# New planner ranks, an earlier first input and an early Tanh table in a four-layer kernel on one Trainium2 core

## The chip, the core and the metric

The kernel runs on one core of one Trainium2 chip. The metric is the device time of one execution in microseconds (us); lower is better. The time of before is the median of three runs.

The core's engines have queues of their own and meet through semaphores: TensorE (PE, matmuls and transposes), VectorE (DVE), ScalarE (ACT), GpSimd (POOL) and SyncE (SP, which here issues nearly all transfers).[...]

## What is computed

32 batches of a 256 x 256 block x pass through four layers. All numbers are fp32.

```python
# layer 0: a block conditioned on a scalar t
h = silu(noise_encoding(t) @ W1 + b1) @ W2 + b2
scale, shift = h @ Wsc + bsc, h @ Wsh + bsh
o = silu(scale * layer_norm(x, gamma, beta) + shift) @ W_in + b_in      # norm over the whole block
x = silu(scale * layer_norm(o, gamma, beta) + shift) @ W_out + b_out + x
# layer 1: attention, 16 heads of 16, with a bias [32, 16, 256, 256] and a key mask
x = ln(x) * (1 + ada_scale) + ada_shift                # ada from an integer token per batch
p = softmax(q @ k.T / 4 + attention_bias, masked)
x = x + (p @ v) @ Wo + bo
x = x + gelu2((ln(x) * g2 + beta2) @ W1 + b1) @ W2 + b2  # 256 -> 1024 -> 256
# layer 2: one step of a stencil equation: first and second differences along both axes
f = relu(f + dt * df)
# layer 3: causal attention of 16 heads, then a feed-forward with exact gelu, gated
y = x + gate * (transformer_block(x) - x)
```

## The kernel before

All weights stay on the chip. Each batch is worked on as two halves of 128 rows. One batch is some 390 matmuls and transposes for TensorE. An attention layer has four units of four heads: `scores` multiplies q and k of four heads in four row strips of the array (32 rows each, tile names sc <- k_t, nq), VectorE adds the bias or the causal mask and takes the minimum (pr, mn), ScalarE takes the exponential and its sum. `turned` transposes the probabilities (tr <- ident, pr), VectorE and ScalarE copy them out (pt). `values` multiplies them with v in four column strips (mm <- pt, L1v or L3v). A matmul thus runs in one of three shapes: the full array, 32 rows, or 32 columns. In layer 1 the bias (nb) comes in by 16 transfers per batch, and GpSimd subtracts it from the mask.

The order of work is not written out. A class `Order` (lines 69 to 383) records every operation of every batch first, with a rank, `order.now`, and its tiles. `arrange` then plans all engines at once with a table of costs: when an engine falls free, the ready operation with the lowest rank is taken. `emit` writes all engines' operations in the planned order, so every instruction of the recorded part bears line 382. The chip keeps that order on each engine.

What sets the ranks: `trace` (line 1155) walks a batch's layer as a generator and advances `order.now` by the yielded steps times `PACE`, starting from `b * PERIOD + START[layer] + EDGE.get((b, layer))` (line 1169), and adds `SHIFT[layer][step]` for each step. What else sets the choice: `EARLIER` moves TensorE operations by the kind of their output tile (line 252); `STAY` (line 302) is added to an operation that would change the array's shape; `FRESH` (line 306) is added on top when that change leads to a two-pass matmul (any fp32 matmul that is not a transpose) on the full array; `CAPS` limits the PSUM tiles of each kind in flight; `SLACK` (line 375) is a time that the plan adds before TensorE may use another engine's result.

```python
                    if e == "pe" and units[u][2][0]["length"][1] != shape:
                        rank += self.STAY
                        if units[u][2][0]["length"][1] != (P, P):
                            rank -= self.PAIR if shape != (P, P) else 0.0
                        elif units[u][2][0]["length"][3] == 2:
                            rank += self.FRESH
```

The plan's `TABLES` tells which function table ScalarE needs: Sin; Tanh and Exp together; Gelu.

The prologue (lines 542 to 652) has rank -1000: it loads the constants through SyncE's queue in the order of the code, computes the sine and cosine encodings on VectorE and ScalarE, and from them the conditioning of all 32 batches in three chained products (`conditioning`, line 606: a matmul group, a copy, a transpose, an addition of the bias): W1 with a silu, W2, then scale and shift (wss). Bias vectors are loaded as rows (as_rows) and transposed. The first batch's x is loaded at line 559, behind W2 and wss. `layer_0` (line 990) takes the block's mean and variance with two one-column matmuls (`block_stats`, line 759), then the scaled silu and two products.

Of the kernel before, what the change touches and what calls it, by code (L numbers as in the profile page):

```python
# [16 lines left out]
AF = mybir.ActivationFunctionType  # L17
# [21 lines left out]

PERIOD = 86.0
START = (-61.8, 0.0, 116.9)
PACE = (1.55, 1.23, 1.08)
EDGE = {(0, 0): 14.4, (0, 1): -5.0, (0, 2): 5.8, (1, 0): -19.0, (1, 1): -3.8, (1, 2): -0.2, (2, 0): -27.1, (2, 1): -2.0, (2, 2): -1.1, (3, 0): 12.3, (3, 1): 0.4, (3, 2): 0.3, (4, 0): 5.2, (4, 1): 2.3, (4, 2): 0.6, (27, 0): -1.1, (27, 1): -1.0, (27, 2): 0.5, (28, 0): 1.7, (28, 1): -0.3, (28, 2): -2.0, (29, 0): 2.1, (29, 1): -0.1, (29, 2): -2.1, (30, 0): -11.1, (30, 1): 5.7, (30, 2): -4.5, (31, 0): -16.9, (31, 1): 1.9, (31, 2): 15.4}
SHIFT = (
    {0: -93.0, 1: -33.6, 2: -27.5, 3: -32.8, 4: -14.7, 5: -56.4, 6: -42.3, 7: -28.3, 8: 23.1},
    {0: -9.7, 1: -80.2, 2: -10.3, 3: -1.7, 4: 2.7, 5: 8.8, 7: -7.0, 8: 14.7, 9: -90.2, 11: 7.3,
     12: 21.2, 13: -0.4, 14: 4.0, 15: -1.3, 16: 11.4, 17: 5.1, 19: 4.8, 20: 10.4, 21: 46.1, 22: 16.4,
     23: -8.7, 24: -13.1, 25: -30.4, 26: -2.4, 27: -90.0, 28: 8.3, 29: -134.0, 30: -0.4, 31: -13.2,  # L50
     32: -34.6, 33: 0.8, 34: -0.3, 35: 7.7, 36: -2.9, 37: -8.0},
    {0: -1.1, 1: -32.9, 2: -9.3, 3: 27.2, 4: 23.9, 5: -25.6, 6: -48.6, 7: -36.4, 8: -12.9, 9: 6.6,
     11: 3.0, 12: 15.4, 13: -32.5, 15: -6.5, 16: 20.0, 17: -2.0, 18: 6.6, 19: -0.5, 20: 0.4, 21: -82.2,
     23: 9.0, 24: 7.5, 25: 0.1, 26: -11.0, 27: -38.3, 28: 12.2, 29: 7.0, 30: 30.4, 31: 3.6, 32: -8.7,
     33: -46.1, 34: 4.4, 35: 2.3, 36: -58.5, 37: -16.3, 38: -59.7, 39: 18.0, 40: -15.2, 41: 12.6},
    {0: -24.5, 1: -13.3, 2: 6.7, 3: -84.2, 4: 42.8},
)
NORM = 8.0
LAND = 3.0
# [5 lines left out]
class Order:  # L65
# [11 lines left out]
    TURN = 92.0  # L77
    FIRST = {(32, P): 107.0, (P, 32): 27.0, (P, P): 107.0}
    APART = 120.0
    SLACK = 50.0  # L80
    SEEN = {(32, P): 165.0, (P, 32): -16.0, (P, P): 165.0}
    CAPS = {"sc": 8, "tr": 7, "mm": 7}
    EARLIER = {"sc": 29.6, "mm": -2.0, "tr": 6.2}
    STAY = 5.0
    FRESH = 1.0
    PAIR = 0.0
    PORT = 0.05
    TABLES = {AF.Sin: 0, AF.Tanh: 1, AF.Exp: 1, AF.Gelu: 2}
# [128 lines left out]
    def arrange(self):  # L217
# [5 lines left out]
        turns = defaultdict(list)  # L223
        room = dict(self.CAPS)
        first = {}
        for u, (engine, rank, xs) in enumerate(units):
# [6 lines left out]
            for t in {t.name: t for x in xs for t in x["tiles"]}.values():  # L233
                f = first.setdefault(t.name, u)
                if f == u:
                    room[t.tag] = t.bufs or t.tag_meta.bufs
                    count[t.tag] += 1
                    if t.source_name in self.CAPS:
                        count[t.source_name] += 1
# [10 lines left out]
        for u, (engine, rank, xs) in enumerate(units):  # L250
            name = next((t.source_name for x in xs for t in x["tiles"] if t.source_name in self.CAPS), "")
            ranks.append((rank - (self.EARLIER.get(name, 0.0) if engine == "pe" else 0.0), u))
        for us in turns.values():
# [15 lines left out]
        def may(u, at):  # L269
            ready_at[u] = max(ready_at[u], at)  # L270
            wait[u] -= 1
            if not wait[u]:
                heapq.heappush(coming[units[u][0]], (ready_at[u], u))
                heapq.heappush(events, ready_at[u])
# [6 lines left out]
        while todo:  # L281
# [6 lines left out]
            for e in self.ENGINES:  # L288
# [6 lines left out]
                for k, heap in ready[e].items():  # L295
# [5 lines left out]
                    if e == "pe" and units[u][2][0]["length"][1] != shape:  # L301
# [3 lines left out]
                        elif units[u][2][0]["length"][3] == 2:  # L305
                            rank += self.FRESH
                    if k[1]:
# [66 lines left out]
                for v in after[u]:  # L374
                    may(v, own if units[v][0] == e and x["method"] != "dma_start" else end + self.HOPS[units[v][0]] + (self.SLACK if units[v][0] == "pe" else 0.0))

# [54 lines left out]
def kernel(ctx: ExitStack, tc: tile.TileContext, io, out, n_batch=B):  # L431
    nc = tc.nc
    order = Order()
    pe, dve, act, pool, sync = (
        order.engine(name, eng)
        for name, eng in (
            ("pe", nc.tensor), ("dve", nc.vector), ("act", nc.scalar), ("pool", nc.gpsimd), ("sync", nc.sync)
        )
    )
# [17 lines left out]
    def rows(ap):  # L457

        return ap.rearrange("(c p) n -> p c n", p=P)
# [37 lines left out]
    def mm_tile(shape):  # L497
        return psum_tile(shape, "mm")
# [22 lines left out]
    def turned_vectors(tag, names, eng):  # L521
        vectors, n_rows = {}, 0
        for name in names:
            n = io[name].shape[0] // P
            vectors[name] = slice(n_rows, n_rows + n)
            n_rows += n
        as_rows = sb.tile([n_rows, P], F32, tag="nq0", name="as_rows")
        for name, at in vectors.items():
            eng.dma_start(as_rows[at], io[name].rearrange("(c p) -> c p", p=P))
        pm = mm_tile([P, n_rows])  # L530
        pe.transpose(pm, as_rows, ident[0:n_rows, 0:n_rows])
        cols = ctile(tag, [P, n_rows])
        dve.tensor_copy(cols, pm)
        return cols, {name: cols[:, at] for name, at in vectors.items()}

    def load_x(b):
        x = sb.tile([P, C2, D], F32, tag="x", name="x")
        sync.dma_start(x, rows(io["x"][b]))
        return x
# [9 lines left out]
    )  # L549
    w1 = sb.tile([P, 4 * E], F32, tag="t2", name="l0w1", bufs=3)  # L550
    sync.dma_start(w1, io["L0_cond_W1"])
    i_b = sb.tile([P, B], I32, tag="nq1", name="i_b")
    sync.dma_start(i_b, io["itok_B_34_63"].partition_broadcast(P))
    w2 = sb.tile([P, 4, 4 * E], F32, tag="hid", name="l0w2", bufs=1)
# [1 line left out]
    wss = sb.tile([P, 2, 4, D], F32, tag="pt", name="l0wss", bufs=3)  # L556
    sync.dma_start(wss[:, 0], rows(io["L0_cond_Wsc"]))
    sync.dma_start(wss[:, 1], rows(io["L0_cond_Wsh"]))
    first_x = load_x(0)
    gb = []  # L560
    for n in ("gamma", "beta"):
        t = sb.tile([P, C2, D], F32, tag="l2", name="l0gb", bufs=4)
# [16 lines left out]
    def cosine(dst, a, r, parts=slice(0, P)):  # L579

        dve.tensor_scalar(a, r, -1.0, None, ALU.mult)
        dve.tensor_tensor(a, a, r, ALU.max)
        dve.tensor_scalar(a, a, -1.0, math.pi / 2, ALU.mult, ALU.add)
        act.activation(dst[parts], a[parts], AF.Sin)

    small = sb.tile([P, 16, B], F32, tag="pr", name="encodings", bufs=10)
    x0, r0, n0, a0, enc, x1f, r1, n1, a1, emb0, emb1 = (small[:, i] for i in range(11))
# [8 lines left out]
    reduced(r1, n1, x1f)  # L596
    act.activation(emb0, r1, AF.Sin)
    cosine(emb1, a1, r1)

    def silu(dst, zh, th, z):  # L600

        dve.tensor_scalar(zh, z, 0.5, None, ALU.mult)
        act.activation(th, zh, AF.Tanh)
        dve.scalar_tensor_tensor(dst, th, 1.0, zh, ALU.add, ALU.mult)

    def conditioning(dst, weights, src, bias):


        pm = mm_tile([P, P])
        with order.together():  # L610
            for k in range(len(weights(0))):
                for j in range(4):
                    pe.matmul(
                        pm[j * B : (j + 1) * B, :], lhsT=src[:, k, :], rhs=weights(j)[k],
                        start=k == 0, stop=k == len(weights(0)) - 1,
                    )
        by_batch = sb.tile([P, P], F32, tag="h_t", name="by_batch")
        dve.tensor_copy(by_batch, pm)
        pm = mm_tile([P, 4, B])
        pe.transpose(pm.rearrange("p j b -> p (j b)"), by_batch, ident)  # L620
        dve.tensor_tensor(dst, pm, bias.unsqueeze(2).broadcast_to([P, 4, B]), ALU.add)
# [6 lines left out]
    part = lambda j: slice(j * P, (j + 1) * P)  # L628
    conditioning(h1, lambda j: [w1[:, part(j)]], enc.unsqueeze(1), vector["L0_cond_b1"])
    silu(h1s, zh, th, h1)  # L630
    conditioning(h2, lambda j: [w2[:, k, part(j)] for k in range(4)], h1s, vector["L0_cond_b2"])
    both = cols0[:, 8:12]
    conditioning(mod0, lambda j: [wss[:, j // 2, k, part(j % 2)] for k in range(4)], h2, both)
# [17 lines left out]
    sync.dma_start(parity, io["c_parity"])  # L651
    order.now = START[0] + 5.0
    _, more = turned_vectors(
# [501 lines left out]
    def trace(n, gen, layer, start, pace):  # L1155
        i = 0
        while True:
            order.now = start + SHIFT[layer].get(i, 0.0)
            step = next(gen, None)
            if step is None:  # L1160
                break
            start += step * pace
            i += 1

    trace(3 * n_batch, loads(), 3, START[1] + 25.0, 1.0)
    res = {}
    for b in range(n_batch):
        for i, layer in enumerate((layer_0, layer_1, layers_23)):
            trace(3 * b + i, layer(b, res), i, b * PERIOD + START[i] + EDGE.get((b, i), 0.0), PACE[i])
    with tc.manual_schedule():  # L1170
# [34 lines left out]
```

## Time and profile before

| | |
|---|---|
| median of three runs | 2665.15 us (2664.05 to 2667.85) |
| the profiled execution | 2665.54 us |
| its span, first to last instruction | 2663.7 us |
| mean granted TensorE clock | 0.989 of full speed |
| TensorE idle from 0 to 95 us | 34.2 us |
| TensorE idle from 300 to 2450 us | 2.4 us |
| TensorE idle in the last 64 us | 17.0 us |
| bytes moved | 169.69 MB, 64 GB/s in the mean, 207 GB/s over the first 95 us |

The profile comes from one execution. Times in its rows are in us. A row of the timeline gives the start from the beginning of the span, the length, the engine, the code line, the operation, the tiles written and read, the size and how many like it follow each other; a bracket tells idle time before it and what ended it. TensorE's rows overlap, because matmuls are pipelined: the distance from start to start is what one costs. A fp32 matmul that is not a transpose leaves two records. A row of the stretches gives the stretch, its length, then the busy time of PE, PE's weight loads, DVE, ACT and POOL with their counts, then the granted clock of TensorE, the busy share of the 16 DMA engines and GB/s.

### The profile page before, as it was taken

To read this page: it belongs to the slowest core of one execution; us is meant where nothing else is said; L and a number is where in the kernel's file an instruction comes from. 1 tells how busy PE (TensorE), PEld (TensorE's weight loads), DVE (VectorE), ACT (ScalarE), POOL (GpSimd) and SP (SyncE) were. 2 spreads that over 40 slices of the span, in tenths; PEclk is the share of its full clock that TensorE was granted. 3 is DMA by queue.
4 is the path that set the end of the run, shared out by engine and by line. 5 is a ranking of instruction groups with operands and counts; after the bars stand their busy time and mean duration, and the time that the engine had idled before them with its cause. 6 is when DMAs were issued, how large, how long until landed. Compare 5 with 4: busy or idle time off the path is not lost.

```text
span 2663.7 us, 60400 instructions
## 1 busy us (share of the span) xinstructions
PE 2600.2 (98%) x20462; PEld 2118.4 (80%) x20462; DVE 2122.1 (80%) x7627; ACT 1920.1 (72%) x6120; POOL 1565.0 (59%) x1960
## 2 busy tenths in 40 slices
PE   5999999999999999999999999999999999999997
PEld 4777888888888888888888888888888888888775
DVE  5887888878878877878878878877878887887853
ACT  2677777877777877777777777877777877777854
POOL 3865676555676555576555677555576555676420
PEclk7999999999999999999999999999999999999998
DMA  7321122212122212122212122212122211122100
GB/s 243 110 60 59 42 73 69 70 49 66 45 70 70 70 49 66 46 70 69 70 49 65 43 73 70 69 49 66 46 69 69 70 57 57 42 69 64 45 5 9
DMA packets 177064, 169.69 MB, mean 64 GB/s; under 512 B 19514, under 2 KB 175220, under 8 KB 176756
## 3 DMA queue, kind: packets, MB, share of 16 engines
q1 hardware_dynamic: 176720, 165.82, 20.2%
q8 instruction: 163, 2.67, 0.4%
q14 instruction: 145, 1.19, 0.1%
q10 hardware_dynamic: 36, 0.01, 0.0%
HBM read 157.40 MB, written 8.39 MB: 62 GB/s over the span
## 4 chain that ended last, share of the span: by engine, by line
PE 91%; DVE 3%; ACT 2%; DMA 1%; POOL 1%; issue 1%; SPq 0%; ACTq 0%; POOLq 0%; DVEq 0%
PE mm L382 68%; PE tr L382 14%; PE sc L382 9%; DVE pr L382 1%; ACT hid L382 1%; ACT pr L382 1%; DMA x<-in_x_dram 1%; POOL nb L382 0%; DMA nb<-in_fside_Bx16xSxS_dram 0%; DVE pt L382 0%; ACT L382 0%; POOL rstd L382 0%; DVE gd L382 0%; DMA L1wo<-in_L_cond_Wo_dram 0%; DVE st L382 0%
## 5 line engine op out<-in xcount | busy, mean ns | idle before, releaser
L382 ACT ACTIVATE pr<-pr,mn 128x256 f32<-128x256 f32 (+1 forms) x2048 | 966.9, 478 | 93.0 <-DVE mn L382 91.8
L382 POOL TENSOR_TENSOR nb<-mask_f,nb 128x512 f32<-128x512 f32 x512 | 693.3, 1378 | 114.7 <-DMA nb<-in_fside_Bx16xSxS_dram 101.9
L382 PE MATMUL tr<-ident,pr 128*128 128x128 f32 x3584 | 508.5, 276 | 5.4 <-ACT pr L382 1.8
L382 PEld LDWEIGHTS tr<-ident,pr 128*128 128x128 f32 x3584 | 419.5, 143 | 85.8 <-ACT pr L382 29.1
L382 DVE CUSTOM_DVE_ANT_0 pr<-sc,nb 128x256 f32<-128x256 f32 x1024 | 388.0, 414 | 25.3 <-POOL nb L382 14.0
L382 ACT ACTIVATION_READ_ACCUMULATOR pr<-pr,mn 128x1 f32 x2048 | 398.0, 194 | 0.0
L382 DVE COPY pt<-tr 128x512 f32<-128x512 f32 (+1 forms) x512 | 311.3, 615 | 72.9 <-PE tr L382 72.3
L382 POOL TENSOR_SCALAR hid<-hid 128x256 f32<-128x256 f32 x256 | 100.0, 405 | 433.4 <-ACT hid L382 433.1
L382 DVE CUSTOM_DVE_ANT_0 pr<-sc,causal 128x128 f32<-128x128 f32 (+1 forms) x1024 | 299.3, 352 | 38.5 <-PE sc L382 37.2
L382 PE MATMUL sc<-k_t,nq 32*128 32x256 f32 (+1 forms) x4096 | 269.5, 375 | 0.1
L382 ACT COPY pt<-tr 128x512 f32<-128x512 f32 (+1 forms) x512 | 261.4, 526 | 10.9 <-PE tr L382 6.0
L382 PE MATMUL mm<-L3w,hid 128*128 128x256 f32 x1024 | 241.5, 385 | 10.1 <-ACT hid L382 10.0
L382 PE MATMUL mm<-h_t,L3w 128*128 128x256 f32 x1024 | 247.6, 382 | 1.5 <-DVE h_t L382 1.4
L382 PE MATMUL mm<-h_t,L1w 128*128 128x256 f32 x1024 | 248.9, 381 | 0.0
L382 PE MATMUL mm<-L1w,hid 128*128 128x256 f32 x1024 | 239.0, 380 | 0.1
L382 PEld LDWEIGHTS sc<-k_t,nq 32*128 32x128 f32 x4096 | 163.3, 185 | 73.0 <-issue 25.7
L382 PEld LDWEIGHTS mm<-L3w,hid 128*128 128x128 f32 x1024 | 190.6, 193 | 35.1 <-ACT hid L382 11.9
L382 POOL COPY wide<-rs 128x256 f32<-128x256 f32 x128 | 53.3, 416 | 281.3 <-DVE rs L382 131.8
L382 PEld LDWEIGHTS mm<-L1w,hid 128*128 128x128 f32 x1024 | 186.6, 190 | 23.3 <-issue 1.2
L382 PEld LDWEIGHTS mm<-h_t,L3w 128*128 128x128 f32 x1024 | 184.2, 191 | 22.9 <-DVE h_t L382 2.5
L382 PEld LDWEIGHTS mm<-h_t,L1w 128*128 128x128 f32 x1024 | 183.7, 190 | 23.3 <-issue 1.8
L382 ACT ACTIVATE t<-x,shift,rstd 128x256 f32<-128x256 f32 x128 | 67.2, 590 | 148.8 <-DVE shift L382 148.8
(173 smaller groups left out, 4997.7 us busy)
## 6 DMA issues: line engine op xcount, KB each, us to landing
nb<-in_fside_Bx16xSxS_dram SPq DMA_DIRECT2D x512, 256.0 KB
x<-in_x_dram SPq DMA_DIRECT2D x32, 256.0 KB
out_dram<-d SPq DMA_DIRECT2D x32, 256.0 KB
mask<-in_mask_Bx1xSxS_bk_dram SPq DMA_DIRECT2D x32, 64.0 KB
L1w<-in_L_cond_W_dram SPq DMA_DIRECT2D x2, 1024.0 KB
L3w<-in_L_cond_W_dram SPq DMA_DIRECT2D x2, 1024.0 KB
l0w<-in_L_cond_W_dram SPq DMA_DIRECT2D x1, 1024.0 KB
g_b<-in_L_cond_B_grid_dram SPq DMA_DIRECT2D x3, 256.0 KB
```

Of the source, the lines that this page charges most:

```text
L382: call(*args, **kwargs)
```

## The change

Nothing in the computation changes. x of the first batch is loaded directly behind W1 instead of behind wss. One activation is added, a Tanh of one column behind the last cosine, whose output nobody uses. The second and third conditioning products, and what is recorded behind them in the prologue, get the rank -960 instead of -1000; layer 0 of the first batch gets about -1070 (its EDGE), so its statistics rank ahead of them. All other ranks are replaced, SLACK doubles, FRESH goes from 1 to 8, and the limits for score and other PSUM tiles fall by one. In the instruction orders that follow from it, every engine's queue is rearranged through all 32 batches; the number of instructions of each kind on each engine stays, but for that one activation, and the number of table loads on ScalarE is 65 in both.

```diff
-PERIOD = 86.0
-START = (-61.8, 0.0, 116.9)
-PACE = (1.55, 1.23, 1.08)
-EDGE = {(0, 0): 14.4, (0, 1): -5.0, (0, 2): 5.8, (1, 0): -19.0, (1, 1): -3.8, (1, 2): -0.2, (2, 0): -27.1, (2, 1): -2.0, (2, 2): -1.1, (3, 0): 12.3, (3, 1): 0.4, (3, 2): 0.3, (4, 0): 5.2, (4, 1): 2.3, (4, 2): 0.6, (27, 0): -1.1, (27, 1): -1.0, (27, 2): 0.5, (28, 0): 1.7, (28, 1): -0.3, (28, 2): -2.0, (29, 0): 2.1, (29, 1): -0.1, (29, 2): -2.1, (30, 0): -11.1, (30, 1): 5.7, (30, 2): -4.5, (31, 0): -16.9, (31, 1): 1.9, (31, 2): 15.4}
+PERIOD = 85.9
+START = (-60.6, 0.0, 116.2)
+PACE = (1.29, 1.23, 1.08)
+EDGE = {(0, 0): -1009.2, (0, 1): -5.2, (0, 2): 1.9, (1, 0): -49.5, (1, 1): -2.6, (2, 0): -9.3, (2, 1): -5.2, (2, 2): -0.7, (3, 0): 0.6, (3, 1): 0.5, (3, 2): -1.4, (4, 0): -18.2, (4, 1): 2.8, (4, 2): 0.6, (27, 0): -14.4, (27, 1): -6.5, (28, 0): -7.6, (28, 1): -3.2, (28, 2): -2.7, (29, 0): -18.9, (29, 1): 3.1, (29, 2): 30.9, (30, 0): 6.8, (30, 1): -0.5, (30, 2): 24.0, (31, 0): -17.2, (31, 1): 8.1, (31, 2): -22.4}
 SHIFT = (
...
 )
...
-    SLACK = 50.0
+    SLACK = 100.0
     SEEN = {(32, P): 165.0, (P, 32): -16.0, (P, P): 165.0}
-    CAPS = {"sc": 8, "tr": 7, "mm": 7}
-    EARLIER = {"sc": 29.6, "mm": -2.0, "tr": 6.2}
+    CAPS = {"sc": 7, "tr": 7, "mm": 6}
+    EARLIER = {"sc": 32.7, "mm": -1.2, "tr": 6.9}
     STAY = 5.0
-    FRESH = 1.0
+    FRESH = 8.0
...
     w1 = sb.tile([P, 4 * E], F32, tag="t2", name="l0w1", bufs=3)
     sync.dma_start(w1, io["L0_cond_W1"])
+    first_x = load_x(0)
     i_b = sb.tile([P, B], I32, tag="nq1", name="i_b")
...
     sync.dma_start(wss[:, 1], rows(io["L0_cond_Wsh"]))
-    first_x = load_x(0)
     gb = []
...
     cosine(emb1, a1, r1)
+    act.activation(a1[:, 0:1], emb1[:, 0:1], AF.Tanh)
...
     silu(h1s, zh, th, h1)
+    order.now = -960.0
     conditioning(h2, lambda j: [w2[:, k, part(j)] for k in range(4)], h1s, vector["L0_cond_b2"])
```

SHIFT is replaced in all its entries: four tables of 9, 35, 39 and 5 numbers that move a layer's steps by a few tens, for example step 21 of layer 1 from 46.1 to 142.1.

## The prediction

> **What bounds the kernel now.** I read the page's busy times first, then busy time by stretches of the span, then the timelines of TensorE and ScalarE in one steady batch, and last the timeline of TensorE at the end.
>
> The page, and the stretches (PE busy is the second number of a row):
>
> ```profile
> PE 2600.2 (98%) x20462; PEld 2118.4 (80%) x20462; DVE 2122.1 (80%) x7627; ACT 1920.1 (72%) x6120; POOL 1565.0 (59%) x1960
> ```
>
> ```profile
> 0.00:95.00 95.00, 60.78 (x415) 43.59 (x416) 58.26 (x219) 34.71 (x102) 47.00 (x64) 0.82 0.66 207
> ...
> 300.00:1200.00 900.00, 899.94 (x7156) 738.24 (x7155) 738.36 (x2666) 675.71 (x2155) 548.65 (x688) 1.00 0.20 61
> ...
> 2537.00:2664.00 127.00, 105.53 (x670) 81.84 (x668) 59.69 (x222) 62.30 (x196) 22.66 (x36) 0.90 0.02 7
> ```
>
> From 300 to 1200 us TensorE is idle for 0.06 us in 900. So two things can move the time: how long TensorE's own stream takes, and the gaps in it at both ends and wherever a new order opens one. No work is removed; the program has 12606 matmuls and transposes before and after.
>
> What one costs, I take from starts in the timeline of TensorE in a steady batch:
>
> ```profile
> 1187.63 1.03 PE L382 MATMUL mm<-L3wv,h_t 128*128 128x256 f32 x4
> 1188.59 0.94 PE L382 MATMUL sc<-k_t,nq 32*128 32x128 f32 x16
> 1189.45 1.13 PE L382 MATMUL mm<-L3wv,h_t 128*128 128x256 f32 x4
> 1190.52 0.94 PE L382 MATMUL sc<-k_t,nq 32*128 32x128 f32 x16
> 1191.38 0.66 PE L382 MATMUL mm<-ident,t 128*128 128x128 f32 x4
> 1191.88 0.49 PE L382 MATMUL tr<-ident,pr 128*128 128x128 f32 x3
> ...
> 1193.07 0.82 PE L382 MATMUL tr<-ident,pr 128*128 128x128 f32 x6
> ```
>
> A fp32 matmul of 256 columns shows as two records and follows the one before after 0.432 us when nothing changes. The two of the first row take 0.96, so going over from the full array (128*128) to a quarter of its rows (32*128) costs 0.093. The same two in the third row take 1.07: coming back costs another 0.104. A transpose takes 0.109 in a row of its kind and 0.165 as the first after a score or value group, so coming back to a transpose costs 0.056. These starts repeat within 2 ns over the run. With such spacings all 12606 instructions take 2558 us. I call the rest of the span, 105.4 us, lost; followed along the records, it is 53.6 at 95 us, 60.2 at 300, 64.6 at 2450, 67.2 at 2537 and 105.4 at the end.
>
> **The change, part by part. TensorE's order.** FRESH 1 to 8 makes the planner reluctant to come back from the small-tile shapes to a two-pass matmul; SLACK, CAPS, EARLIER and the new shifts rearrange the rest. I counted changes of shape in both instruction orders. Full array to score or value group: 327 before, 287 after, 40 x 0.093 = 3.7 us. Back to a two-pass matmul: 99 to 58, 41 x 0.104 = 4.3 us. Back to a transpose: 228 both times. Transpose to two-pass matmul, 0.0027 each: 727 to 619, 0.3 us. A one-column matmul (statistics) ahead of a transpose, 0.034: 57 to 36, 0.7 us; ahead of a two-pass matmul, 0.083: 65 to 64, 0.1. Together **-9.1 us**, all of it on the engine that is never idle.
>
> **One new wait per batch.** Now ScalarE in the same microsecond:
>
> ```profile
> 1185.01 1.07 ACT L382 ACTIVATE t<-xm,shift,rstd 128x256 f32<-128x256 f32 x2
> 1187.83 0.84 ACT L382 ACTIVATE k_t<-mm,cols 128x256 f32<-128x256 f32 x2 [1.75 <-PE mm L382]
> 1188.69 1.28 ACT L382 ACT_TABLE_LOAD   x1
> 1189.98 0.40 ACT L382 ACTIVATE pr<-pr,mn 128x128 f32<-128x128 f32 x1
> ...
> 1190.38 0.49 ACT L382 ACTIVATE pr<-pr,mn 128x256 f32<-128x256 f32 x1
> 1190.78 0.19 ACT L382 ACTIVATION_READ_ACCUMULATOR pr<-pr,mn 128x1 f32 x1
> ...
> 1191.77 0.51 ACT L382 ACTIVATE pr<-pr,mn 128x256 f32<-128x256 f32 x1
> ```
>
> Here the two t activations run before k_t, in an idle gap. In the changed order they stand between k_t and the table load in 21 batches, so every exponential behind them starts 1.07 us later. Behind them on ScalarE stand the load, four exponentials and two L3v copies; TensorE waits for the exponentials. The first transposes started at 1191.88, and the sum behind the second exponential had been read at 1190.78 + 0.19 = 1190.97: 0.91 to spare, so 0.16 short after. The transposes of the next tile (first at 1193.07) had their data at 1192.37 (exponential at 1191.77, its read 0.41 later, 0.19 long), 0.70 to spare; the changed order brings them 0.08 closer to the scores, so 0.70 - 0.08 - 1.07 = 0.45 short. A later wait in the same batch does not add, it is the same lateness. 21 x 0.45 = **+9.5 us**. Bounds: the lateness could vanish if the scores themselves come later (0), or grow by a second such place that I don't see (0.8 each): 0 to 17.
>
> This is where the Trainium skill speaks against the change. The row shows the load at 1.28 us and the exponential 0.01 later, with nothing after it. "ScalarE: Activation LUTs", section "What ACT_TABLE_LOAD costs", adds about 1.38 us of drain to every switch of the table. By the row the wait is 0.45 a batch; by the page it would be 0.45 + 1.38 = 1.83, since in the changed order an activation runs right up to the load (38 us in all). But k_t runs right up to it before as well, and no drain shows, so I take the row.
>
> **The prologue.** The added Tanh is one 128x1 activation, by the nearest row (64x32) 0.23 us. But it stands behind a Sin again: the changed order on ScalarE is Sin, Tanh (for the hidden layer), Sin, Tanh, four loads where two stood. The two added loads and the activation, 2 x 1.28 + 0.23 = 2.8 us, lie between the hidden layer's tanh (done at 11.6) and the next ScalarE work at 18.86, a gap of 7.2 us: nothing, and 2.8 at most if that gap were gone. (At the end two loads are saved, 65 in all both times.)
>
> x behind W1 costs no bytes; it moves SyncE's later issues by one, 0.43 us, and the 1 MB of W2 behind a wait for t_b's landing (4.18), 1.5 us later than now. x should land near 6 (W1 lands at 4.91, 256 KB more at 350 GB/s) instead of 12.90, so TensorE's wait of 2.47 us for it goes, and VectorE's statistics no longer hold back the hidden layer (11.05 to 12.90). What is late next: both gamma and beta now stand ahead of the W2 matmuls on TensorE, and beta lands around 14.4 (the second bias row's issue at 14.38 waits for it), so those matmuls start near 15.4 against 14.83. Then the bias rows (as_rows, 22.87 now, about 0.5 earlier since the second x was moved behind them) stand ahead of the transpose that gives the scale. The first input matmul (27.25) gains about 0.5 us. And after it the order is fixed: L1's Wo matmul, which waits for its transfer until 32.68, ahead of the means. The second x now travels ahead of Wo (0.7 us at the 360 GB/s of that stretch), so Wo lands no earlier. Hence the first stages keep their time; the gain is that 1.9 us more of TensorE's work (the second batch's input matmuls) stands ahead of the first L1 transposes at 50.17. **-2 us**; bounds -5 (the bias transfers of the first L1 attention, where 12 us are lost from 65 to 95, also fall better) and +4 (they fall worse; SyncE's queue there is reordered too). From 95 to 300 I take the 6.5 us lost as unchanged, +-4.
>
> **The end.** The last rows of TensorE before the change:
>
> ```profile
> 2599.81 1.89 PE L382 MATMUL mm<-h_t,L3wq 128*128 128x256 f32 x8
> ...
> 2628.59 2.56 PE L382 MATMUL mm<-L3wo,ctx_t 128*128 128x256 f32 x8
> 2634.88 0.93 PE L382 MATMUL mm<-ident,t 128*128 128x128 f32 x4 [3.73 <-ACT t L382]
> 2636.45 8.73 PE L382 MATMUL mm<-h_t,L3w 128*128 128x256 f32 x32 [0.64 <-DVE h_t L382]
> 2649.34 8.86 PE L382 MATMUL mm<-L3w,hid 128*128 128x256 f32 x32 [4.15 <-ACT hid L382]
> ```
>
> The last batch runs alone there: 24 us of the last 64 are lost. In the changed order, batch 30's last feed-forward (14.3 us of TensorE work) stands inside the last batch's attention. I take as milestone the end of the last batch's L1 Wo (2537.04), with 88.5 us of TensorE work left before and 96.0 after. The last batch's chain from there, in the changed order: two waits of 4.0 and 1.4 us to its feed-forward; 19.1 us of dense work and 1 us for the last gelu; 25.4 us to its L3 input transposes (22.6 now; VectorE's score work of batch 30 now stands in it); 2.2 to Q. That makes 53.1. Q to Wo takes 28.8 now, 30.5 with eight more ScalarE activations (0.42 each, half hidden). Wo to the first feed-forward matmul takes 7.9 now; batch 30's gelu with its table load (1.28 + 1.91) and 6.9 us of matmuls stand in it, 10.0. From there 27.2 now, 25.9 without a load of its own. Sum 119.5; with 1.5 for what I have overlooked, 121.0. That leaves 121.0 - 96.0 = 25.0 lost, against 126.7 - 88.5 = 38.2: **-13.2 us**. Bounds -19 and 0. On the way to the milestone the order is tighter than now (the first L1 feed-forward matmul stands right behind its input): +0.5, between 0 and 3.
>
> **Sum.** -9.1 + 9.5 - 2 + 0.5 - 13.2 = -14.3. The profiled execution took 2665.54 us (span 2663.7); the median of the runs shown is 2665.15, 0.4 below. 2665.15 - 14.3 = 2650.9, so 2651.
>
> **Rivals.** *The end gives nothing*: batch 30's ScalarE work (3.4 of bias activations, 3.2 of load and gelu) and VectorE work falls into the last batch's chain and costs the 13 us that TensorE gains. For it: both are serial there. Against it: ScalarE is busy 28 of the last 64 us. -1.1, 2664. *The ScalarE wait doesn't arise*, since small latenesses elsewhere already absorb it: -23.8, 2641. *The ScalarE wait is much longer*: one mechanism, the t activations and the load ahead of the first exponential in 21 batches. The other terms give -23.8, so it turns the result to slower by 0.2% from (23.8 + 5.3) / 21 = 1.39 us a batch; at the 1.83 of the drain it makes +14.6, 2680. For it: TensorE has no idle time that would take it up. Against it: the load row. *The change doesn't do what it says*: x early buys nothing, since Wo's landing decides; that is in my sum.
>
> **Numbers.** A measurement of this kernel can tell about 0.2%, 5.3 us, from no change. Forecast 0.58, end gives nothing 0.14, no wait 0.20, long wait 0.08. Faster by over 0.2% (below 2659.8): nearly all of the forecast, all of no wait and some of the first rival, 0.82; within: 0.12; slower: 0.06. The range runs from 2635 (no wait, and the end at its better bound) to 2664 (the end gives nothing).
>
> **What would show it.** TensorE's starts: 287 entries into small shapes at +0.093; if they cost differently, the first step is wrong. Around each third-layer attention, t between k_t and the table load, and transposes waiting about 0.45 for ACT pr; the row 300:1200 would then show some 5 us idle. Wo landing near 32.5 and the first L1 transposes near 50. 96 us of TensorE work in the last 121. The prediction is wrong if TensorE waits over 1 us per batch, or if the last batch's Q starts more than 72 us before the end.

## The result and the profile after

The median of 20 runs is 2671.64 us (2668.5 to 2676.18) against 2665.37 us for the kernel before in the same comparison: a ratio of 1.0024, 95% interval 1.0018 to 1.0030. The change makes the kernel slower by 0.24%, where the forecast was 0.5% faster. The profiled execution has a span of 2670.6 us (before 2663.7), a difference of 6.9 (7.0 in the table below, whose rows are rounded).

First the page's busy times, then the stretches of the span, in the columns of the rows of before:

```profile
PE 2612.4 (98%) x20462; PEld 2120.9 (79%) x20462; DVE 2130.2 (80%) x7627; ACT 1921.1 (72%) x6121; POOL 1553.7 (58%) x1960
```

```profile
0.00:95.00 95.00, 65.73 (x424) 44.87 (x425) 58.24 (x220) 37.39 (x106) 48.63 (x66) 0.82 0.65 208
...
300.00:1200.00 900.00, 896.22 (x7071) 732.65 (x7071) 737.74 (x2617) 661.77 (x2110) 540.69 (x681) 1.00 0.20 61
```

TensorE is idle for 3.8 us in the 900, against 0.06 before. That looks small. But look at the counts: 7071 records instead of 7156 in the same 900 us, although the new order's spacings are shorter. The busy column doesn't show where the time goes, because the drawn ends of matmuls are modelled and a drawn row covers most of a short pause.

The starts do show it. Take the spacings that the prediction read from the kernel before, lay them along each kernel's own order on TensorE, and call lost what is left over between one start and the next. Summed over the whole trace, this is the ledger:

| us | before | after | difference | predicted |
|---|---|---|---|---|
| TensorE's own stream (12606 instructions at their spacings) | 2558.3 | 2548.9 | -9.3 | -9.1 |
| lost from 0 to 300 | 60.2 | 61.1 | +0.9 | -2 |
| lost from 300 to 2450 | 4.4 | 35.5 | +31.1 | +9.5 |
| lost from 2450 to the end | 40.8 | 25.1 | -15.7 | -12.7 (the end -13.2, the way there +0.5) |
| sum | 2663.7 | 2670.6 | +7.0 | -14.3 |

One row is far off, and it is large enough to turn the sign. Of the 35.5 us in it, 24.3 are at one place, where the kernel before loses less than 0.1: the first three tiles of probability transposes (three transposes each) of the third-layer attention, nearly all of it in 19 batches. This is TensorE there, in the batch that stands for the one shown of before:

```profile
1198.49 1.03 PE L382 MATMUL mm<-L3wv,h_t 128*128 128x256 f32 x4
1199.45 0.94 PE L382 MATMUL sc<-k_t,nq 32*128 32x128 f32 x16
...
1202.86 0.33 PE L382 MATMUL tr<-ident,pr 128*128 128x128 f32 x1
1203.36 0.44 PE L382 MATMUL tr<-ident,pr 128*128 128x128 f32 x2 [0.16 <-ACT pr L382]
1203.63 1.03 PE L382 MATMUL mm<-h_t,L1wq 128*128 128x256 f32 x4
1204.50 0.98 PE L382 MATMUL tr<-ident,pr 128*128 128x128 f32 x4
1205.64 0.44 PE L382 MATMUL tr<-ident,pr 128*128 128x128 f32 x2 [0.16 <-ACT pr L382]
```

From 1202.86 to 1203.36 one transpose takes 0.50 where 0.11 is its spacing: 0.39 lost, of which the bracket calls 0.16 idle. It had itself started 0.12 late (4.37 behind the first row, 4.25 before). The six transposes that followed each other before now break after the fourth. From the first row to the fifth of them, at 1205.64, it takes 7.15; the kernel before did the same in 5.88 (1187.63 to 1193.51, which is the row at 1193.07 and four spacings of 0.109). So 1.27 us were lost on this way, and 0.06 behind it, since the transpose that follows a pause starts 0.06 late. The page's table of waits, restricted to 300 to 2450, has 5.0 us in 29 waits for these exponentials, and the ledger 24.3. The Trainium skill, "Perfetto Trace Analysis", section "Tensor Engine Instruction (MATMUL, LD_WEIGHTS)", says that TensorE's end in a trace is estimated. That fits what the rows show: a single transpose is drawn with 0.33 us where its spacing is 0.11, and four fifths of the waits show no idle time.

ScalarE and VectorE in the same microseconds:

```profile
1198.69 0.84 ACT L382 ACTIVATE k_t<-mm,cols 128x256 f32<-128x256 f32 x2 [1.97 <-PE mm L382]
1199.91 1.09 ACT L382 ACTIVATE t<-xm,shift,rstd 128x256 f32<-128x256 f32 x2 [0.38 <-DVE shift L382]
1201.02 1.28 ACT L382 ACT_TABLE_LOAD   x1
1202.32 0.40 ACT L382 ACTIVATE pr<-pr,mn 128x128 f32<-128x128 f32 x1
```

```profile
1199.01 0.68 DVE L382 SCALAR_TENSOR_TENSOR th<-th,y 128x512 f32<-128x512 f32 x1
1199.61 0.33 DVE L382 TENSOR_SCALAR shift<-mv,rstd 128x1 f32<-128x1 f32 x2
```

The order is the predicted one: k_t, t, load, exponentials. But t doesn't follow k_t directly. It waits 0.38 us for shift, which stands behind th on VectorE in the new order. The first exponential starts 3.83 us behind the first row of the TensorE block (1198.49), against 2.35 before (1189.98 less 1187.63): 1.48 us late, not 1.07.

Seven of the 19 batches are like this one. In eleven others shift comes earlier, t waits 0.15 us for it, and the first exponential is 1.25 us late (1282.67, with the TensorE block from 1279.07); one batch lies between.

```profile
1280.26 1.09 ACT L382 ACTIVATE t<-xm,shift,rstd 128x256 f32<-128x256 f32 x2 [0.15 <-DVE shift L382]
```

The last exponential that the six transposes need is the second of the third tile. Its sum is read here, in the kernel before and in the changed one (the batch shown first):

```profile
1193.06 0.19 ACT L382 ACTIVATION_READ_ACCUMULATOR pr<-pr,mn 128x1 f32 x1
```

```profile
1205.40 0.19 ACT L382 ACTIVATION_READ_ACCUMULATOR pr<-pr,mn 128x1 f32 x1
```

At the end the profile shows what was predicted, batch 30's feed-forward inside the last batch's attention:

```profile
2607.98 1.89 PE L382 MATMUL mm<-h_t,L3wq 128*128 128x256 f32 x8
...
2636.72 1.56 PE L382 MATMUL mm<-L3wo,ctx_t 128*128 128x256 f32 x6 [0.37 <-DVE ctx_t L382]
2639.49 5.45 PE L382 MATMUL mm<-L3w,hid 128*128 128x256 f32 x24 [1.20 <-ACT hid L382]
...
2656.88 8.79 PE L382 MATMUL mm<-L3w,hid 128*128 128x256 f32 x32 [2.87 <-ACT hid L382]
```

Where TensorE stood idle before between Wo and the last feed-forward (3.73 for t), it now does w2 of batch 30. From the end of the last batch's layer-1 Wo matmul (2552.25) the rest takes 118.4 us with 96.0 us of TensorE work in it.

### The profile page after: what moved, and what is told of

It reads as the page before. It is cut to its first block, busy times and chain, and to the rows that moved or that the text cites. A ratio compares the mean times of both kernels' runs of the same rounds, so it can differ in the third digit from the quotient of the medians.

```text
span 2670.6 us, 60377 instructions
## 1 busy us (share of the span) xinstructions
PE 2612.4 (98%) x20462; PEld 2120.9 (79%) x20462; DVE 2130.2 (80%) x7627; ACT 1921.1 (72%) x6121; POOL 1553.7 (58%) x1960
## 4 chain that ended last, share of the span: by engine, by line
PE 53%; POOL 17%; DVE 14%; ACT 8%; DMA 4%; issue 3%; SPq 1%; POOLq 0%; ACTq 0%; DVEq 0%
PE mm L382 38%; PE tr L382 9%; PE sc L382 6%; POOL nb L382 5%; ACT pr L382 4%; DMA nb<-in_fside_Bx16xSxS_dram 3%; POOL d L382 2%; POOL rstd L382 2%; DVE dd L382 2%; DVE pr L382 2%; DVE nq L382 1%; DVE x L382 1%; POOL offset L382 1%; ACT L382 1%; POOL cmf L382 1%
## 5 line engine op out<-in xcount | busy, mean ns | idle before, releaser
L382 PEld LDWEIGHTS tr<-ident,pr 128*128 128x128 f32 x3584 | 412.9, 142 | 103.1 <-ACT pr L382 46.1
L382 ACT ACTIVATION_READ_ACCUMULATOR pr<-pr,mn 128x1 f32 x2048 | 412.6, 201 | 0.0
L382 DVE DVE_READ_ACCUMULATOR2_ANT mn<- 128x1 f32 x2048 | 168.9, 82 | 0.0
```

Source lines behind the costliest of these rows:

```text
L382: call(*args, **kwargs)
```

## The experiments

Theory A: all of the surplus at the transposes is lateness of ScalarE's exponentials, made of t's length and t's wait for shift; what exceeds the spare of the tightest tile (the time by which its data are early) goes one to one into TensorE's wait. Rivals: something else in the new order, such as VectorE's minima or fewer matmuls between the transposes, sets the waits (theory B); or the prediction's own 0.45 us a batch holds and the rest comes from elsewhere.

Some edits are made behind the plan: `emit` sorts by the planned start, so changing the start of single operations moves these alone. Each experiment but the sixth and the tenth leaves TensorE's order through the steady part as it was. Ratios are to the kernel before, run in the same comparison.

**1. The table load taken out of the way.** A tiny exponential ahead of k_t makes ScalarE load the table in its idle gap.

```diff
+            elif func(x) == AF.Exp and table == AF.Gelu:
+                table, j = AF.Exp, i
+                while is_t(acts[j - 1]) or is_k(acts[j - 1]):
+                    j -= 1
...
+                    more.append({"call": (call, (self.tick[0], self.tick[1], AF.Exp), {}), "start": acts[j]["start"] - 0.01})
```

> The changed kernel with one 128x1 exponential added in 22 batches, ahead of k_t on ScalarE, where that engine waits 1.97 us for TensorE; its output is used by nobody. The table load then happens there and not behind t; all other instructions keep their order. Theory A (the waits of 1.24 us a batch at the first three groups of probability transposes come from ScalarE being late by t, its wait for shift, and the load): 1.28 of the 1.47 us of lateness go, the transposes wait for less than 0.1 us a batch, 2671.6 - 23 = 2648. Theory B (the waits are set by something else in the new order, VectorE's minima or the thinner cover of matmuls between the transposes): 2671, within 2 us. If the added load does not fit into the gap and delays k_t, some 0.3 us a batch come back: 2655.

Measured: 2646.65 us, ratio 0.9931 (0.9919 to 0.9944). Theory A holds, theory B falls, and 25 us less than the changed kernel is more than 0.45 us a batch could give back. ScalarE, then TensorE:

```profile
1182.77 1.28 ACT L400 ACT_TABLE_LOAD   x1
1184.06 0.20 ACT L400 ACTIVATE tick<-mhalf 128x1 f32<-128x1 f32 x1
1184.67 0.84 ACT L400 ACTIVATE k_t<-mm,cols 128x256 f32<-128x256 f32 x2 [0.40 <-PE mm L400]
1185.75 1.09 ACT L400 ACTIVATE t<-xm,shift,rstd 128x256 f32<-128x256 f32 x2 [0.24 <-DVE shift L400]
1186.74 0.39 ACT L400 ACTIVATE pr<-pr,mn 128x128 f32<-128x128 f32 x1
```

```profile
1184.47 1.03 PE L400 MATMUL mm<-L3wv,h_t 128*128 128x256 f32 x4
...
1188.71 0.49 PE L400 MATMUL tr<-ident,pr 128*128 128x128 f32 x3
...
1189.91 0.82 PE L400 MATMUL tr<-ident,pr 128*128 128x128 f32 x6
```

The load and the tick fill 1.5 us in which ScalarE was waiting for TensorE anyway. k_t still starts when TensorE has it. The six transposes follow without a pause. From 300 to 2450, 11.4 us are lost instead of 35.5. This kernel is faster than the one before and the changed one.

**2. t behind k_t in the kernel before.** The opposite: the one suspected move, alone.

```diff
+            if is_t(x) and is_t(acts[i + 1]) and is_k(acts[i + 2]) and is_k(acts[i + 3]):
+                for j in range(2):
+                    acts[i + j]["start"] = acts[i + 3]["start"] + 0.1 + 0.1 * j
```

> The kernel before with only the two t activations moved from ahead of k_t to behind it on ScalarE in 25 batches; TensorE, VectorE, GpSimd and the transfers keep their orders. Lateness 1.07 us, since shift is there early in this order. The prediction's step (spare 0.91 at the first and 0.70 at the next tile, nothing behind it): 0.37 us a batch, +9, 2674. Theory A (the third tile of the group has only 0.15 us to spare, 1193.40 less 1193.25, so nearly all of the 1.07 falls on TensorE, and each interruption costs 0.06 more): 0.95 to 1.1 a batch, +24 to +27, 2690. Theory B (ScalarE's order does not matter): 2665.

Measured: 2686.67 us, ratio 1.0079 (1.0065 to 1.0092), 20 us slower. This kernel does not compute the same: the layer-1 norm reads xm after the feed-forward's bias was added to it, and in the last two batches the transposes ahead of layer 3 read t before it is written. The ledger has 18.4 us at the first three tiles in 23 batches, 0.80 a batch: twice the prediction's step, somewhat less than theory A's range. That range was too high for two reasons: two activations in a row delay the load by 0.97 us, not by 1.07, and the expectation took the fourth transpose for the tight one where it is the fifth, 0.11 later.

**9. The same move, with everything reading what it read before.** Only the 23 layer-1 norms are moved, and GpSimd's addition to xm is placed behind them.

```diff
+                for j, y in enumerate(adds.get(x["call"][1][1].tensor.name, [])):
+                    y["start"] = max(y["start"], acts[i + 3]["start"] + 0.3 + 0.1 * j)
```

> The second experiment once more, with t moved only in the 23 batches where it is the layer-1 norm, and with GpSimd's addition to xm behind it, so that every operation reads what it reads in the kernel before. Theory A: 23 x 0.80 = 18.4 us of waits at the first three tiles as in the second experiment, 2685, within 2. The prediction's step (0.37 a batch): 2674. If the 20 us of the second experiment came from what else had moved there: 2667.

Measured: 2685.24 us, ratio 1.0076 (1.0063 to 1.0090). TensorE in this kernel:

```profile
1201.93 0.98 PE L398 MATMUL tr<-ident,pr 128*128 128x128 f32 x4
1203.08 0.44 PE L398 MATMUL tr<-ident,pr 128*128 128x128 f32 x2 [0.16 <-ACT pr L398]
```

The six transposes break after the fourth here too. A tile has three of them, and the first needs only the tile's first exponential: the fourth opens the third tile, and the two behind it wait for that tile's second exponential. Of the 18.4 us, 12.0 fall there, 5.1 at the second tile and 1.3 at the first.

**3. shift ahead of th in the changed kernel.**

```diff
+            if tile_of(x).startswith("th0") and tile_of(dves[i + 1]).startswith("shift"):
+                for j in (1, 2):
...
+                    dves[i + j]["start"] = x["start"] - 0.3 + 0.1 * j
```

> The changed kernel with shift taken ahead of th on VectorE in 20 batches; nothing else moves. t then has shift when k_t ends and does not wait 0.38 us for it. Theory A (this wait is part of the lateness, and lateness beyond the spare goes one to one into TensorE's wait): 20 x 0.37 = 7.4 us less, 2664. The prediction's step, which knew only the 1.07 of t itself: no change, 2671. Theory B: 2671. If th, 0.5 us later, is waited for, it comes out above 2671.

Measured: 2663.31 us, ratio 0.9991 (0.9984 to 0.9997), some 8 us less than the changed kernel. The ledger's waits at the first three tiles fall from 24.3 to 17.1 us, nearly all of the difference at the first tile, where 8.5 become 1.4. In the seven batches with the long wait for shift the exponentials come 0.50 us earlier and TensorE loses 0.50 less, in the eleven others 0.27 and 0.28: one to one.

**4. The prologue alone.** The kernel before with x behind W1, the rank -960, the Tanh and the first batch's rank.

> The kernel before with the prologue's part of the change alone: x directly behind W1, the rank -960, the early Tanh, the first batch's layer 0 ranked at about -1070. On TensorE 22 of 12606 places differ, all in the first 100 us. The prediction had -2 us for the prologue, of which 1.9 by work put ahead of the first layer-1 transposes, which this kernel does not have; so by its working 0 here, 2665. If the early x is worth something by itself: down to 2662. If the reordered queue of transfers costs: up to 2669.

Measured: 2665.7 us against 2666.18, ratio 1.0000 (0.9992 to 1.0009). x arrives at 6.16 instead of 12.90 and buys nothing:

```profile
6.16 1.09 PE L382 MATMUL mm<-ident,x 128*128 128x128 f32 x4 [6.16 <-DMA x<-in_x_dram]
...
32.69 1.10 PE L382 MATMUL mm<-L1wo,cols 128*128 128x256 f32 x4 [1.57 <-DMA L1wo<-in_L_cond_Wo_dram]
```

The matmul that waits for Wo starts at 32.69 (before 32.68), with the early x as without it.

**5. Control: the early table load in the kernel before.** The same tiny exponential ahead of k_t as in the first experiment, here in 28 batches (there 22).

> Control: the kernel before with the same added exponential ahead of k_t, in 28 batches. Theory A (the early table load is worth only what TensorE waits for late exponentials, and in this order it doesn't): 2665.5, within 2 us. Rival (an earlier table load is worth something in any order, so the first experiment says nothing about the new order): 20 us less, 2645.

Measured: 2665.03 us, ratio 1.0001 (0.9992 to 1.0009). The early load is worth nothing in this order, where TensorE does not wait for the exponentials. The gain of the first experiment belongs to the new order.

**6. The old ranks at the end.** The changed kernel with the early load, and the EDGE entries of batches 27 to 31 as before.

> The changed kernel with the early table load of the first experiment, and the ranks (EDGE) of batches 27 to 31 put back to those of before; TensorE's order differs from nominal 1900 us on and ends as before the change does: batch 30's feed-forward stands again ahead of the last batch's attention, 81.6 us of TensorE work are left at the last batch's layer-1 Wo (96.0 with the new ranks, 88.5 before). To be compared with the first experiment (2646.7). The prediction's step (work inside the last batch's serial chain is free, 12.7 in all): the chain takes about as long as before, 126.7 from Wo, with 7 us less work in it than before: 17 to 24 us more, 2664 to 2671. Rival (the end gives nothing, the gain of the first experiment is all in the steady part): 2647.

Measured: 2666.75 us, ratio 1.0006 (0.9998 to 1.0014), 20 us more than the first experiment. From 2450 to the end 44.9 us are lost against 23.2 there. So the end's rearrangement is worth something, and the first experiment's gain needs it. These 20 us are not its worth against the kernel before: with the old ranks the new order leaves 81.6 us of TensorE work behind the last batch's layer-1 Wo, the kernel before 88.5. Against that one the table's -15.7 counts.

**7. Early load and shift together**, the edits of 1 and 3.

> The changed kernel with both the early table load and shift ahead of th. Theory A (lateness below the spare of the transposes costs nothing): the early load has already brought it below, so the 0.37 us a batch that shift was worth alone are worth nothing more: 2646.7, within 2. Rival (every 0.1 us that ScalarE is earlier shows in the end): 2639.

Measured: 2647.2 us, ratio 0.9932 (0.9920 to 0.9945), no better than the early load alone. What was worth 8 us by itself is worth nothing once the exponentials are within the spare.

**8. t behind k_t, and the early load on top**, in the kernel before. The last two batches' transposes ahead of layer 3 read t before it is written, as in the second experiment.

> The kernel before with t behind k_t as in the second experiment (2686.7) and the early table load on top; GpSimd's addition to xm is placed behind t, so that t reads what it reads in the kernel before. Theory A (the exponentials' lateness costs the time): lateness 0.97 less 1.28 is below zero, so all 20 us come back: 2666, within 2. Rival (t itself comes too late for its own transposes, mm from ident and t, or for what follows from them): 2686.

Measured: 2666.19 us, ratio 1.0000 (0.9992 to 1.0008). All 20 us come back, though t is as late as in 2 (0.93 us behind the first row of the TensorE block in both). So it is not t that is waited for, but the exponentials behind it.

**10. FRESH alone.**

```diff
-    FRESH = 1.0
+    FRESH = 8.0
```

> The kernel before with FRESH at 8 and nothing else changed. In the planned order this leaves 327 entries into small shapes and 99 returns to a two-pass matmul, as before. So by counting: no change, 2666. The prediction named FRESH as what makes the shape changes fewer; if that were so, some of 8 us should go: 2660.

Measured: 2668.15 us, ratio 1.0006 (0.9998 to 1.0015): no difference. FRESH isn't what makes the shape changes fewer. The other way round, the changed kernel planned with FRESH at 1 has 289 entries into small shapes and 63 returns to two-pass matmuls in its planned order, against 287 and 58. Nearly all of the difference to the 327 and 99 of before is made by what else is new in the ranks and limits; which part of it was not tried.

## Why the prediction was wrong, point by point

- *TensorE's order, -9.1*: right, -9.3 by the same spacings. In both kernels score and value groups, with the changes of shape around them, keep the spacing read from before within 0.002 us in the mean, next to whatever they stand. What the prediction said of its cause, that FRESH does it, was wrong (experiment 10).
- *One new wait per batch, +9.5 with bounds 0 to 17*: the mechanism was right, the size wrong, and this is the failed step. It measured 24.3 us at the three tiles, 1.2 a batch instead of 0.45. Two terms were mis-sized. First, "every exponential behind them starts 1.07 us later": the two activations alone make it 0.97 (experiments 3 and 9), and t's wait for shift makes it 1.25 in eleven batches and 1.48 in seven; VectorE's new order was not read at this place. Second, "0.70 to spare" at "the transposes of the next tile". The row of six transposes covers two tiles, and only the first of them was checked. The other's second transpose started at 1193.07 + 4 x 0.109 = 1193.51, and its exponential's sum was read at 1193.06 + 0.19 = 1193.25: 0.26, and with the 0.05 from data to start (1205.40 + 0.19 = 1205.59 to 1205.64 in the changed kernel) 0.21 to spare. So 1.48 - 0.21 = 1.27 us are short, and with the 0.06 of the restart 1.33: what the starts show in this batch. The same sum gives 1.10 for a lateness of 1.25, where 1.11 was measured, and 0.82 for the 0.97 of experiment 9, where 0.83 was measured in 22 of its 23 batches. "A later wait in the same batch does not add" is right where the first wait is the tightest; the tightest was the third, and it took what the other two had left. A third term, that "the changed order brings them 0.08 closer to the scores", does not appear in these batches: from the first row of the block to the row of six transposes it is 5.44 us in the kernel before (1187.63 to 1193.07) and in the first experiment (1184.47 to 1189.91).
- *Drain after a table load*: left out, rightly. The Trainium skill, "ScalarE: Activation LUTs", section "What ACT_TABLE_LOAD costs", would add about 1.38 us of drain to the switch; here the load follows t at once (1199.91 + 1.09 to 1201.02), the exponential follows 0.02 after the load ends (1201.02 + 1.28 to 1202.32), and in the first experiment the tick follows 0.01 after it.
- *Other waits of the steady part*: put at nothing, and 7 us more than before: 11.2 us (35.5 less 24.3) against 4.4. They are scattered: 2.8 us at the last tile of the same attention in 7 batches, 2.7 at the stencil, 1.8 ahead of the third layer's Q, and smaller ones. Which constant (the limits of tiles in flight, SLACK, the shifts) makes them was not tried, and the cause stays open; the first experiment still has most of them.
- *The row 300:1200 with some 5 us idle*: it shows 3.8 and would have passed as a confirmation. The view can't measure this. The other mark, over 1 us per batch, was reached.
- *Prologue, -2*: +0.9 to 300 us. That an early x buys nothing by itself was right (experiment 4). The first L1 transposes came at 52.62, not near 50: the input matmuls of both batches now stand ahead of them, and TensorE's clock was low there (below); in the first experiment, with the same order, they came at 50.45.
- *The end, -12.7 in all*: -15.7. The chain took 118.4 us where 121.0 was predicted, but two misses offset each other in that, which is luck: up to Q it took 55.7 (2552.25 to 2607.98) where 53.1 was predicted (54.6 with the 1.5 for what was overlooked), and from Q to the end 62.6 where 66.4 was. And one order varies here: in experiment 9, with the end's order of the kernel before, the chain took 123.3 us where it took 126.9.
- *The rivals*: the long ScalarE wait happened, the one given 8 in 100, but not by the drain that it was priced with. It was to turn the result from 1.39 us a batch. At the three tiles it is 24.3 / 21 = 1.16, so it did not turn the result alone.

With the measured 24.3 in place of 9.5, the sum becomes +0.5: no change, where it had said clearly faster. The failed step thus takes the forecast gain away. From there to the +7.0 of the table: the scattered waits (+7), the prologue (+3), the end (-3).

## What to carry to other kernels

When work is moved in front of a producer, look for the smallest spare among all its consumers, not for the first one: a row of the timeline that groups six instructions has six due times. Measure waits of a pipelined engine by the distance of starts, since its busy time rose here by 12 us while its own work fell by 9. And if a function table has to be loaded, put the load where its engine waits anyway, but expect a gain only if somebody waits for what comes behind it.

## What the runs showed that was not expected

A short pause costs TensorE more than the pause. After each wait for an exponential the next transpose starts 0.06 us later than its spacing, as after a change of shape; with three pauses in a batch that is 0.18 us, and it is contained in the 1.2.

In the prologue the granted clock differs between profiled executions with the same order on TensorE. The same eight matmuls, in the changed kernel and in the first experiment:

```profile
46.43 3.78 PE L382 MATMUL mm<-th,l_win 128*128 128x256 f32 x8 [1.72 <-DVE th L382]
```

```profile
46.05 1.99 PE L400 MATMUL mm<-th,l_win 128*128 128x256 f32 x8 [1.72 <-DVE th L400]
```

From 46 to 56 us the granted clock was 0.68 in the one and 1.00 in the other. The Trainium skill, "TensorE: Matmul & The Clock Gate", section "Part 1: The HAM clock gate", tells of a gate that passes half of the clock's pulses when the array was little used; 3.78 against 1.99 fits that. The changed kernel and the first experiment lost 61.1 and 58.8 us up to 300, so about 2 us there vary between these two executions of one order, and the +0.9 says little.
